# Latent attention with a dense layer on one core: rotary rows off GpSimd, block 0's side work dealt by a table

## The chip, the core and the metric

The kernel runs on one core of a Trainium2 chip. A core has five engines that run side by side and wait for each other through semaphores: TensorE (PE in the profile; its weight loads are PEld), VectorE (DVE), ScalarE (ACT), GpSimd (POOL) and SyncE (SP), which here only issues transfers. TensorE reads SBUF and writes PSUM; GpSimd works on SBUF alone in this kernel. The metric is the device time of one execution in microseconds. Shown for the kernel before are three runs: 1577.43, 1583.23 and 1586.42 us, median 1583.23.

## The reference, cut to what matters

One sequence of 2048 tokens with 512 features goes through an attention layer whose queries and keys come from low-rank latents, then through a dense layer. Both are followed by a residual and a layer norm.

```python
cq  = rms_norm(x @ w_qa.T, q_a_ln_w)              # 2048 x 384
q   = (cq @ w_qb.T)                               # 16 heads of 128 (nope) + 64 (pe)
q_pe = q_pe * cos + rotate_half(q_pe) * sin
ckv = x @ w_kva.T                                 # 2048 x (128 + 64)
k_pe = rope(ckv[..., 128:])                       # one, shared by all heads
kv  = rms_norm(ckv[..., :128], kv_a_ln_w) @ w_kvb.T   # per head 128 (k_nope) + 128 (v)
scores = (q_nope . k_nope + q_pe . k_pe) * 192 ** -0.5, causal
out = softmax(scores) @ v @ w_o.T
x = layernorm(x + out)
x = layernorm(x + x @ (weight * scale_weight[:, None]).T + bias)
```

The kernel never forms the keys and values of a head. It multiplies `w_qb` by the key half of `w_kvb` (`weights_q`), so a query meets the normalized latent itself, and it does the value half of `w_kvb` together with `w_o` after the softmax. Almost every operand is kept as a high and a low half in 16 bits, so that a product is made of three matmuls (high with high, high with low, low with high).

## The kernel before

**Blocks, pairs, tiles.** The queries are four blocks (b = 0 to 3) of 512. In a block, `units` goes over eight pairs of heads (p), and in a pair over four query tiles of 128 (qt). A tile of block b sees nk = (4b + qt + 1) * 128 keys. In block 0, where nk is at most 512, `pair_scores` makes the scores of both heads at once, takes the maxima (VectorE), the exponentials (ScalarE), and the reciprocal of the sum. `pair_probs` scales them and splits them into high and low halves (`hl`), and a transposing transfer brings them into `PT`. `values` multiplies the latent values by `PT` some tiles later; `lag` says how many tiles (3 in block 0). In blocks 1 to 3, `head_scores` and `head_probs` do the same for one head at a time, with scores in up to two pieces.

**Side work in block 0.** While block 0's tiles run, the rest of the inputs is still to be projected. `rest_of_x` projects the other twelve groups of 128 tokens (`project_x`: products, norm, transposes, store) and then, in `late_keys`, splits the rotated keys for all later blocks. `rest_of_w` prepares the query weights of three further groups of four heads (`weights_q`). Both are generators. Their steps, and those of the fillers (`project_pe` and `project_nope`, which make the next pair's queries), are taken in `units` at fixed places: one filler before each tile's scores, one step of `rest_of_x` in every tile but qt = 1, one step of `rest_of_w` in every tile of the first five pairs.

**Rotary part of the queries.** For a group g of four heads, `rope_products` multiplies and weighs with cosine and sine into `prod`. `rope_split` subtracts and adds (lines 504 and 505), and makes the high half by ScalarE and the low half (lines 507 to 512). `rope_stack` (line 521) then copies 32-row pieces so that the four heads' high and low rows stand under each other: 16 copies of 32x512 for a group. Block 0 gives the copies of the high rows to GpSimd and those of the low rows to VectorE; later blocks give all to GpSimd, except the first group of block 1, which VectorE does.

**Order.** TensorE's order is always the order of the program. In block 0 and to the start of block 3 a scheduler sets the order on VectorE, ScalarE and GpSimd. From the second tile of block 3 on, VectorE and ScalarE too run in program order. SP runs in program order from block 1 on. PSUM in block 0 has two buffers for scores and four (`m`) that all side products share: `ps_kv`, `ps_cq`, their transposes, `ps_wq`, `ps_qn`, `ps_pe`, `ps_tot` and the values' `o`. A product can only start when the buffer four products back has been read.

**Where the change touches.** In `kv_products`, `kvr` is a copy of a product of 256 columns (line 326), and GpSimd multiplies its second half by the cosine and sine table (`rot`, line 331) and adds (`kp`, line 334). `kv_finish` scales by the inverse norm on GpSimd (`nk`, line 340). `project_x` copies the query latent out of PSUM (`nq`, line 422) and scales it on GpSimd (line 424); before block 0's tiles the same is done from PSUM on VectorE (`cq_finish`, line 359). The inverse norm itself is two small GpSimd operations (lines 287 and 288). The low half of the inputs is a GpSimd subtraction (`xl`, line 308).

## Time and profile before

| what | value |
|---|---|
| runs shown, median (lowest to highest) | 1583.23 us (1577.43 to 1586.42) |
| the profiled execution | 1588.19 us, its span 1586.4 us |
| TensorE busy | 1500.4 us, 95% |
| VectorE busy | 1165.4 us, 73% |
| ScalarE busy | 923.7 us, 58% |
| GpSimd busy | 377.2 us, 24% |
| block 0's first scores, first maxima | 52.84 us, 53.71 us |
| block 1's first scores | 282.04 us |
| the last tile's exponentials end, output stage begins | about 1328 us |

The span has four stretches: the preparation up to block 0's first scores (0 to 53 us), block 0 with the side work (53 to 282 us), blocks 1 to 3 (282 to 1328 us), and the output stage (1328 to 1586 us). A line of the profile's groups names the line of the program, the engine, the operation, what is written and read with shapes, how often, the busy time in us and the mean of one in ns, and then the idle time ahead of it with what ended that. A line of the waits names who waited, for whom, the total in us, how often, and the longest. In a table of stretches each engine's busy time and number of instructions stand after the length of the stretch; PEclk is the granted TensorE clock, where 1.00 is full speed.

### The profile page before, as it was taken

What the parts mean: (1) busy time and instruction counts of PE and PEld (TensorE: products, weight loads), DVE (VectorE), ACT (ScalarE), POOL (GpSimd) and SP (SyncE); (2) the same over time, 40 slices, a digit from 0 to 9 for tenths busy, and PEclk for the clock granted to TensorE, in tenths of its full rate; (3) what the DMA queues carried; (4) which work ended last, traced back from release to release, by engine and by line L of the source; (5) the groups of instructions that cost most, each with busy time, mean ns of one, the idle gap of its engine ahead of it and who ended that gap; (6) DMA issues with size and microseconds to landing.
All of it is one profiled execution on the core that took longest, in us unless ns stands there. A gap on an engine that the chain in (4) does not pass through costs nothing. (4 is left out here: it accounts for less than half of the span.)

```text
span 1586.4 us, 24549 instructions
## 1 busy us (share of the span) xinstructions
PE 1500.4 (95%) x9100; PEld 1007.0 (63%) x9100; DVE 1165.4 (73%) x2124; ACT 923.7 (58%) x1668; POOL 377.2 (24%) x490
## 2 busy tenths in 40 slices
PE   8788887999999899999998999999999998999998
PEld 6667654566666566666665666566566666788876
DVE  4767787888878888888886777677677775465554
ACT  5566565666666676767765666666666665311120
POOL 5556531421405404040032400400400000022132
PEclk9999899999999999999999999999999999999999
DMA  5275455698889687978886788688688798433230
GB/s 203 76 181 163 113 128 135 123 173 153 161 180 176 128 170 151 164 150 163 161 189 122 145 154 159 129 154 161 119 153 168 159 228 198 144 118 122 93 113 34
DMA packets 614872, 234.56 MB, mean 148 GB/s; under 512 B 569696, under 2 KB 593248, under 8 KB 614112
## 3 DMA queue, kind: packets, MB, share of 16 engines
q1 hardware_dynamic: 613440, 231.26, 68.0%
q8 instruction: 71, 1.16, 0.3%
q10 hardware_dynamic: 1008, 1.18, 0.3%
q0 software_dynamic: 304, 0.56, 0.2%
q14 instruction: 49, 0.40, 0.1%
HBM read 62.33 MB, written 28.05 MB: 57 GB/s over the span
## 5 line engine op out<-in xcount | busy, mean ns | idle before, releaser
L596 PE MATMUL s<-Kn,qn 128*128 128x512 f16 (+5 forms) x1920 | 466.1, 349 | 20.6 <-ACT pr L648 20.3
L648 ACT ACTIVATE pr<-s,bias,er 128x1024 f32<-128x1024 f32 (+3 forms) x320 | 324.1, 1015 | 227.4 <-DVE bias L642 172.3
L725 PEld LDWEIGHTS <-V 128*128 128x128 f16 x3264 | 321.2, 99 | 94.5 <-issue 20.3
L672 DVE SCALAR_TENSOR_TENSOR hl<-pr,inv,hl 128x1024 f16<-128x1024 f32 (+7 forms) x320 | 350.8, 1110 | 34.4 <-ACT hl L669 28.9
L725 PE MATMUL o<-ring,V 128*128 128x256 f16 x3024 | 361.0, 273 | 0.0
L596 PE MATMUL s<-Kp,pe 128*128 128x512 f16 (+5 forms) x1280 | 342.4, 349 | 0.0
L669 ACT ACTIVATE hl<-pr,inv 128x1024 f16<-128x1024 f32 (+7 forms) x320 | 294.1, 960 | 76.7 <-ACT pr L648 33.9
L633 DVE TENSOR_REDUCE neg<-s 128x1 f32<-128x1024 f32 (+3 forms) x320 | 317.5, 992 | 24.0 <-PE s L596 20.6
L596 PEld LDWEIGHTS <-qn 128*128 128x128 f16 x1920 | 188.4, 98 | 173.8 <-issue 29.7
L596 PEld LDWEIGHTS <-pe 128*128 128x128 f16 x1280 | 125.3, 98 | 107.3 <-issue 1.3
L521 POOL COPY pe<-ph 32x512 f16<-32x512 f16 (+1 forms) x216 | 162.3, 751 | 26.8 <-ACT ph L511 11.8
L1013 PE MATMUL acc<-wvo,oh 128*128 128x512 f32 x448 | 144.8, 404 | 2.0 <-ACT pr L648 2.0
L554 PE MATMUL ps_qn<-cq,wq 128*128 128x512 f16 (+1 forms) x594 | 141.4, 386 | 5.6 <-DVE qn L69 2.8
L504 POOL TENSOR_TENSOR prod<-prod 128x512 f32<-128x512 f32 x15 | 19.0, 1268 | 525.1 <-DVE prod L499 525.1
L660 DVE TENSOR_SCALAR inv<-sums 128x1 f32<-128x1 f32 x128 | 27.1, 212 | 109.6 <-ACT pr L648 109.0
L554 PEld LDWEIGHTS <-wq 128*128 128x128 f16 x594 | 60.0, 101 | 69.6 <-issue 15.3
L1013 PEld LDWEIGHTS acc<-wvo,oh 128*128 128x128 f32 x448 | 83.6, 189 | 23.8 <-issue 4.1
L1013 PE MATMUL acc<-wvo,ol 128*128 128x512 f32 x224 | 88.5, 395 | 0.0
L494 PE MATMUL ps_pe<-cq,wpe 128*128 128x512 f16 (+1 forms) x306 | 69.8, 376 | 4.1 <-DVE nq L359 2.7
L730 ACT ACTIVATE ot<-o 128x256 f32<-128x256 f32 x128 | 48.2, 377 | 36.6 <-PE o L725 35.2
L74 ACT ACTIVATE oh<-o 128x1024 fp32r<-128x1024 f32 x28 | 29.7, 1059 | 64.3 <-PE acc L1013 48.6
L75 DVE TENSOR_TENSOR ol<-o,oh 128x1024 fp32r<-128x1024 f32 x28 | 38.8, 1386 | 37.9 <-ACT oh L74 37.9
(177 smaller groups left out, 1617.6 us busy)
## 6 DMA issues: line engine op xcount, KB each, us to landing
ot_d<-ot SPq DMA_DIRECT2D x128, 128.0 KB, 2.3
o<-ot_d SPq DMA_DIRECT2D x32, 512.0 KB, 3.7
wq<-wq_d SPq DMA_DIRECT2D x30, 384.0 KB, 3.7
wpe<-wpe_d SPq DMA_DIRECT2D x15, 384.0 KB, 3.8
wo<-in_wo_dram SPq DMA_DIRECT2D x4, 1024.0 KB, 5.5
x<-in_x_dram SPq DMA_DIRECT2D x16, 256.0 KB, 4.1
out_dram<-xb SPq DMA_DIRECT2D x16, 256.0 KB, 2.0
xr<-in_xT_dram SPq DMA_DIRECT2D x12, 256.0 KB, 4.3
```

Source lines behind the costliest of these rows:

```text
L75: nc.vector.tensor_tensor(l, ps, h.bitcast(F32), ALU.subtract)
L494: nc.tensor.matmul(ps, w[:, i, lt, x * P : (x + 1) * P], cq[:, k, lt, cols], start=n == 0, stop=n == 3 * LT - 1)
L521: engs[i].tensor_copy(pe[r : r + 32, j, cols], ph[q, i, x, cols])
L554: nc.tensor.matmul(ps, w[:, i, lt, j * P : (j + 1) * P], cq[:, k, lt, cols], start=n == 0, stop=n == 3 * LT - 1)
L596: nc.tensor.matmul(ps[:, :w], lhs, K[:, i, c0 : c0 + w], start=n == 0, stop=n == 4)
L633: nc.vector.tensor_reduce(neg[:, ti : ti + 1], v, axis=AX.XY, op=ALU.max, negate=True)
L648: nc.scalar.activation(pr[:, c0 : c0 + n * w].rearrange("p (a c) -> p a c", a=n), v, AF.Exp, bias=bias, scale=r, accum_out=sums[:, ti : ti ...
L669: nc.scalar.activation(hl[:, 0, c], pr[:, c], AF.Copy, scale=inv)
L672: nc.vector.scalar_tensor_tensor(hl[:, 1, c], pr[:, c], inv, hl[:, 0, c], ALU.mult, ALU.subtract)
L725: nc.tensor.matmul(ps[:, :256], vt[:, i, k % 4, :], v[:, :, l, k, :], start=n == 0, stop=n == 3 * kts - 1)
L730: nc.scalar.activation(ot, ps[:, :256], AF.Copy)
L1013: nc.tensor.matmul(acc, l[:, t, c], state["wvo"][p][:, i, j, :], start=p == 0 and j == 0 and n == 0, stop=p == NPAIR - 1 and j == 1 and n ...
```

## The change

Four things are changed together.

1. `kv_products`, `kv_finish` and `project_x` no longer pass through GpSimd: `rot` is multiplied by VectorE straight from PSUM and `kvr` is half as wide; `nk` is scaled by ScalarE; `nq` is scaled by VectorE from PSUM (`cq_finish`) after the norm is known, instead of copied first. GpSimd keeps the inverse norms, `xl`, and the small additions of `kp`.
2. `rope_split` runs on VectorE in blocks 1 to 3 (additions and low half); block 0 keeps its additions on GpSimd. `rope_stack` becomes a generator. In block 0 and for the first group of block 1, VectorE does all copies at once. In later groups ScalarE copies the high rows and VectorE the low rows, three copies after each head's scores (`move_rows`).
3. Before block 0's tiles: the rotary weights are loaded earlier and their squares taken earlier; each query tile's norm is made by itself; one query product is moved ahead of the column totals; the first products of the next weight group and the next split of x are moved between the two halves of the first queries, from after them; all of these use the four PSUM buffers `x`.
4. In block 0 a table `plan` says for each tile which steps to take (F a filler, X a step of `rest_of_x`, W a step of `rest_of_w`), after its scores; the probabilities of a tile are finished at once instead of after the next tile's scores; values run four tiles behind instead of three.

```diff
 def weights_q(g, direct=None, k="m"):
+    for lt in range(LT if direct is not None else 0):
+        nc.scalar.activation(junk[:, :256], rpe[:, lt], AF.Square, scale=qln[:, lt : lt + 1], accum_out=...)
...
-        kvr = pa2.tile([P, 256], F32, tag="kvr", name="kvr")
-        nc.vector.tensor_copy(kvr, ps[:, :256])
+        kvr = pa2.tile([P, P], F32, tag="kvr", name="kvr")
+        nc.vector.tensor_copy(kvr, ps[:, :P])
...
-        nc.gpsimd.tensor_tensor(rot, kvr[:, P:256].rearrange("p (a d) -> p a d", a=2), csk[:, i], ALU.mult)
+        nc.vector.tensor_tensor(rot, ps[:, P:256].rearrange("p (a d) -> p a d", a=2), csk[:, i], ALU.mult)
...
-        nc.gpsimd.tensor_scalar(nk, kvr[:, :P], rk, None, ALU.mult)
+        nc.scalar.activation(nk, kvr, AF.Copy, scale=rk)
...
-            nq = pa2.tile([P, LT * P], F32, tag="nq", name="nq")
-            nc.vector.tensor_copy(nq, pc)
             rk = inverse_rms(ms)
-            nc.gpsimd.tensor_scalar(nq, nq, rk[:, 1:2], None, ALU.mult)
+            nq = cq_finish(pc, rk[:, 1:2])
...
-    def rope_stack(pe, ph, cols, js, engs):
+    def rope_stack(pe, ph, cols, js, high):
         for j in js:
             q = slice(32 * j, 32 * j + 32)
-            for i in range(2):
-                for x in range(2):
-                    r = 64 * i + 32 * x
-                    engs[i].tensor_copy(pe[r : r + 32, j, cols], ph[q, i, x, cols])
+            for x in range(2):
+                yield high(pe[32 * x : 32 * x + 32, j, cols], ph[q, 0, x, cols])
+                yield nc.vector.tensor_copy(pe[64 + 32 * x : 96 + 32 * x, j, cols], ph[q, 1, x, cols])
+
+    def scalar_copy(dst, src):
+        return nc.scalar.activation(dst, src, AF.Copy)
+
+    stack = []
+
+    def move_rows(n=99):
+        while n and stack:
+            if next(stack[0], None) is None:
+                stack.pop(0)
+            else:
+                n -= 1
...
-        rope_split(b, prod, ph, every, (nc.gpsimd, nc.gpsimd), nc.gpsimd if b else nc.vector)
+        rope_split(b, prod, ph, every, (nc.vector, nc.vector) if b else (nc.gpsimd, nc.gpsimd), nc.vector)
...
+        later_rows = b and (b, g) != (1, 0)
+        stack.append(rope_stack(pe, ph, every, range(4), scalar_copy if later_rows else nc.vector.tensor_copy))
+        if not later_rows:
+            move_rows()
...
+    nc.sync.dma_start(wpe_r, a["wpe"][:, :, 0])
     nc.sync.dma_start(wk0, a["wk"][:, 0:4])
     nc.sync.dma_start(wqb_r, a["wqb"][0])
     nc.sync.dma_start(x_r[1], a["xT"][1])
     nc.sync.dma_start(csk[1], a["csk"][1])
-    nc.sync.dma_start(wpe_r, a["wpe"][:, :, 0])
...
+        def query(hb, i):
+            pc = cq_products(hb, i, x[hb], wqa, "x", msq[hb][:, i : i + 1])
+            return cq_finish(pc, inverse_rms(msq[hb][:, i : i + 1], 1)[:, 0:1])
...
         turn_queries(0, nqs, "x")
+        nqs = [query(1, 0)]
         next(w0)
         key_scales(0, 4)
         exp_scale(0, slice(0, 1))
-        nqs = queries(1)
-        next(w0)
+        nqs.append(query(1, 1))
...
             if hb == 0:
                 for _ in w0:
                     pass
-        next_x(2)
+                for _ in range(LT):
+                    next(w1)
+                next_x(2)
...
+    plan = (
+        ("WWF", "WFX", "WX", "X"),
+        ("FW", "FWF", "FXW", "W"),
+        ("FXW", "FW", "XW", "X"),
+        ("FW", "FWF", "FXW", "W"),
+        ("FXW", "FW", "XW", "X"),
+        ("FX", "FF", "FX", "X"),
+        ("FX", "FX", "X", "X"),
+        ("FX", "FX", "FFX", "X"),
+    )
...
-        lag = min(ring.shape[1] // (2048 * (b + 1)) - 1, 3) if b else 3
+        lag = min(ring.shape[1] // (2048 * (b + 1)) - 1, 3) if b else 4
...
                 if nk <= 512:
-                    fill()
                     pi = pair_scores(pool, b, p, qt, nk)
-                    flush()
                     probs.append(pair_probs(pool, b, p, qt, nk, PT, *pi))
-                    if qt != 1:
-                        next(side[0], None)
-                    if p < 5:
-                        next(side[1], None)
-                    if p + qt == 0:
-                        next(side[1], None)
+                    flush()
+                    for step in plan[p][qt]:
+                        if step == "F":
+                            fill()
+                        else:
+                            next(side[step == "W"], None)
                     run_values(lag)
                     run_values(lag)
...
+                        move_rows(3)
                         if 2 * qt + j in at:
                             fill()
```

## The prediction

> **What bounds the kernel now.** I read the page's engine shares first, then the table of stretches, then TensorE's waits, stretch by stretch, and last the groups and timelines of the operations that the change moves.
>
> ```profile
> PE 1500.4 (95%) x9100; PEld 1007.0 (63%) x9100; DVE 1165.4 (73%) x2124; ACT 923.7 (58%) x1668; POOL 377.2 (24%) x490
> ```
> ```profile
> core 0: us, PE busy (x) PEld busy (x) DVE busy (x) ACT busy (x) POOL busy (x), PEclk, DMA share, GB/s
> 0.00:53.00 53.00, 43.74 (x264) 36.79 (x265) 30.59 (x80) 29.82 (x85) 24.84 (x51) 0.97 0.49 165
> 53.00:201.00 148.00, 122.81 (x800) 94.36 (x797) 106.24 (x226) 93.08 (x269) 87.18 (x129) 0.91 0.52 138
> 201.00:282.00 81.00, 65.07 (x414) 39.98 (x415) 63.22 (x149) 48.10 (x126) 18.60 (x18) 0.90 0.57 134
> 282.00:866.00 584.00, 571.66 (x3658) 358.38 (x3656) 487.81 (x970) 400.92 (x688) 143.51 (x154) 0.99 0.82 160
> 866.00:1328.00 462.00, 447.46 (x2836) 278.97 (x2836) 346.19 (x502) 296.83 (x435) 52.90 (x57) 0.99 0.79 153
> ```
>
> TensorE is the bound, but not everywhere alike. From 282 us on it is busy 98% and 97% of the stretch at a clock of 0.99. In block 0 (53 to 282 us) it is idle for 25.2 + 15.9 us, and its clock is granted at 0.91 and 0.90 only: 13.3 + 8.1 us more in which no work was done. So some 62 of these 229 us are open to better order, and in blocks 1 to 3 only 27 us of 1046. The waits say what is late:
>
> ```profile
> PE o L725 <- DMA PT<-hl: 15.3, 4, 5.1
> PE ps_kv L316 <- POOL xl L308: 6.8, 1, 6.8
> PE ps_kt L379 <- DVE qn L69: 4.4, 1, 4.4
> PE ps_tot L165 <- DVE kvr L326: 4.3, 1, 4.3
> ...
> PE ps_qt L372 <- POOL nq L424: 2.7, 2, 2.4
> PE ps_pe L494 <- DVE nq L359: 2.7, 1, 2.7
> ```
> The four waits for transposed probabilities lie between 219 and 281 us, where the side work has run out; the one for `xl` ends at 60.76 us. GpSimd never bounds the span, but it holds the others up. The same VectorE copy of rotary rows, with GpSimd copying beside it (105 us) and with GpSimd idle (270 us):
>
> ```profile
> L521 DVE COPY pe<-ph x8: 286/492/636, 105.6 to 109.2; 32x512 f16<-32x512 f16 x8
> ```
> ```profile
> L521 DVE COPY pe<-ph x16: 274/284/289, 270.1 to 276.3; 32x512 f16<-32x512 f16 x16
> ```
>
> A copy takes 0.284 us alone and 0.492 beside GpSimd's. In the groups, GpSimd's own price is 0.776:
>
> ```profile
> L521 POOL COPY pe<-ph 32x512 f16<-32x512 f16 x200 | 155.2, 776 | 19.1 <-PE o L725 6.0 <-ACT ph L511 4.7
> L521 DVE COPY pe<-ph 32x512 f16<-32x512 f16 x40 | 16.2, 404 | 0.6
> ```
>
> **The change, part by part.** The sum is made against the profiled execution, 1588.2 us (span 1586.4), which is 5.0 us or 0.3% above the median of the runs, 1583.2.
>
> *Preparation (0 to 53 us).* TensorE's waits there that end on late norms and totals are 1.9 us (totals at 28.03), 2.7 (first rotary product at 36.29) and 1.5 (first weight product at 48.11); the clock of 0.97 costs 1.6. Together 7.7. A query product moved ahead of the totals covers the first; single norms free a PSUM buffer sooner. Against it: two more pairs of small GpSimd operations (0.23 + 0.72 us each), three squares of 0.51 + 0.19 us ahead of the sums they belong to, and on SP the rotary weights (0.39 MB) ahead of four other loads. Between +4 and -7.7; I take -4, about half, since each wait has a second cause close behind.
>
> *First split of x.* `xl` waited behind eight GpSimd copies (55.45, 3.92 us). Now no copy is on GpSimd, the split is asked for a half earlier, and the key product that reads it stands after two tiles' scores. The 6.8 us go, and with them half of the clock lost around 58 to 65 us (0.89 and 0.77 in two stretches of 10 us, 3.4 us). Between 0 and -10.2; I take -9, because some 10 us of TensorE work now stand ahead of that product, and the split needs 2.5 on GpSimd and 1.1 on ScalarE.
>
> *Rest of the first four pairs (to 201 us).* Idle 25.2 - 6.8 = 18.4 us and clock 13.3 - 3.4 = 9.9: 28.3 in all. What is removed: twelve hops of `nq` over GpSimd (1.40 us each), sixteen of `nk` (0.70) and of `rot` (0.46), and 24 + 16 rotary copies. What is added on VectorE: 24 copies of 32x512 at 0.284 and 16 of 32x256 at 0.22 (10.3 us), and `rot` from PSUM, 16 at about 0.28 (4.5, estimated from the 0.42 of 256 columns), less 2.2 for the shorter `kvr`. Its own old copies get cheaper by about the same as this: 24 from 0.46, 16 from 0.44, and other VectorE work that overlaps GpSimd's shrinks too. I put VectorE's net at 0. ScalarE gains 16 `nk` at 0.31 = 5 us, beside 93 busy of 148. The two longest waits (4.3 at 110.90, 4.4 at 182.63) do not vanish by this: both end when VectorE reads a side product behind a run of eight rotary copies (3.86 and 3.54 us); the run is now sixteen, 4.5 us. What helps them is that fewer side products are crowded into a tile. `nq` keeps its PSUM buffer about 1 us longer, until the norm (0.22 + 0.72) is known; queued behind it are the weight product and the values that take the next of the four buffers. Between +8 (three longer runs, twelve longer holds half covered) and -28.3; I take -13.
>
> *Last four pairs (to 282 us).* Idle 15.9 and clock 8.1: 24.0. Probabilities are now finished in their own tile and read four tiles later, so a transfer has some four tiles of 5 us instead of two. A new wait: each transposing transfer must stay back until the values of four tiles before have read the same buffer, late in its own tile; behind it on SP stand stores of `ot` and loads of x and weights. That leaves still more than three tiles. But side work now lies here too, and it brings VectorE and ScalarE work: VectorE is already busy 63 of 81 us. What is late next is the chain maximum, exponential, split, with two score buffers. Between 0 and -24; I take -13.
>
> *Blocks 1 to 3.* Per group VectorE gets two additions (0.69, the price of a 512 column operation, row 499), the low half (1.25) and eight copies (0.284): 4.9 us, for eleven groups 54, and 2.6 for the first. Less what GpSimd's overlap costs VectorE now: I estimate 18 us from durations with and without it. ScalarE gets 88 copies at about 0.63 (its 512 column row): 55 us. Room: VectorE idle 212 us, ScalarE 348 us of 1046. ScalarE also stops waiting for GpSimd's additions, which delay the exponentials at about 991 us and cost TensorE 2.9 us at 999.72. Between -8 (those waits go) and +55 (every ScalarE copy on the path, below); I take +4.
>
> [...]
>
> Sum: -4 - 9 - 13 - 13 + 4 = -35, so 1553 for an execution like the profiled one, 1548 beside the median. I forecast 1552. Output stage unchanged.
>
> **The rivals.** (a) *VectorE takes over block 0.* It is busy 200 us of the first 282 and idle for 82. If its work is unchanged and its idle time shrinks only by what it waits for TensorE and for `nk` now (some 10), the gain is 10 and the blocks give 4 back: 1582, or 1577 beside the median. For it: three bursts of sixteen copies. Against: the waits of the last pairs were for transfers, not for VectorE. (b) *Slower: the copies lengthen the head's loop in blocks 1 to 3.* In block 3 a head's chain, exponential, inverse, split, low half, maximum, bias, closes at 6.6 us (exponentials at 998.37 and 1005.00), as long as TensorE's work for it, and ScalarE's copies enter right before the split, where it waited only 0.53 us. All 88 exposed would cost 55, the sum 1604. It decides from 39 / 0.63 = 62 exposed copies on. Against it: the lag is made up once per pair, where a filler gives TensorE 4 us of other work and VectorE waits again. (c) *Nearly all goes.* All of block 0's loss: -7.7 - 10.2 - 28.3 - 24 + 4 = -66, 1522. Against it: VectorE would be busy nearly throughout.
>
> **How the numbers follow.** The forecast has 0.63, (a) 0.16, (b) 0.11, (c) 0.10. A difference under 0.5% (8 us) can't be told from none here. (a) lies at that edge: 0.05 faster, 0.10 same, 0.01 slower. So faster 0.63 + 0.10 + 0.05 = 0.78, same 0.10, slower 0.12. The range for 8 in 10 leaves out (b) and most of (c): 1527 to 1582; the forecast alone runs from 1535 to 1570.
>
> **What would show it.** Right: block 1's first scores near 244 to 252 us instead of 282; no TensorE wait for transposed probabilities; no wait for `xl` at 60 us; a clock near 0.95 in block 0; VectorE's rotary copies at 0.285 in the mean; blocks 1 to 3 within 10 us of 1046. Wrong: waits of TensorE for VectorE's reads of side products that add up to over 25 us in block 0, which is (a); waits for exponentials well over 20 us after block 0, which is (b).

## The result and the profile after

The changed kernel takes 1594.69 us (median of five executions, 1590.60 to 1596.43) against 1580.63 us for the kernel before on the same chip: a ratio of 1.0081, 95% interval 1.0054 to 1.0108. It is slower by 0.8%, and the prediction of 1552 us, faster by 2%, is wrong on both counts: outside its range and on the wrong side.

The profiled execution is the median one, with a span of 1592.8 us. The engines' busy times on its page:

```profile
PE 1501.2 (94%) x9100; PEld 1007.1 (63%) x9100; DVE 1197.0 (75%) x2304; ACT 982.2 (62%) x1772; POOL 123.4 (8%) x198
```

TensorE's work is the same. GpSimd has lost 254 us of its 377; VectorE has gained 32 and ScalarE 58. The table of stretches of the changed kernel, cut at the same times as the one in the prediction (engines with busy us and instructions, then the granted clock, the DMA share and GB/s):

```profile
0.00:53.00 53.00, 43.59 (x252) 35.31 (x253) 29.06 (x90) 32.12 (x94) 18.90 (x40) 0.94 0.50 172
53.00:201.00 148.00, 129.56 (x848) 98.94 (x848) 113.14 (x281) 101.00 (x290) 38.23 (x66) 0.92 0.59 147
201.00:282.00 81.00, 68.28 (x443) 43.32 (x441) 67.15 (x168) 50.65 (x128) 8.42 (x10) 0.95 0.57 135
282.00:866.00 584.00, 566.20 (x3599) 354.23 (x3598) 497.16 (x1035) 432.47 (x740) 6.39 (x2) 0.99 0.80 157
866.00:1328.00 462.00, 439.50 (x2792) 272.99 (x2791) 352.71 (x525) 304.70 (x446) 0.00 (x0) 0.99 0.78 151
```

Up to 282 us TensorE does 10 us more work in the same time than before: that is the gain. From 282 to 1328 us it is busy 13.4 us less than before (1005.7 against 1019.1), which means idle time that was not there. The same is seen in the times at which each block's first scores start:

| kernel | block 1 | block 2 | block 3 | first output product | end |
|---|---|---|---|---|---|
| before | 282.0 | 508.4 | 849.9 | 1323.7 | 1586.4 |
| after | 264.9 | 512.0 | 852.5 | 1332.8 | 1592.8 |

These are single executions. The one of the kernel before took 1588.2 us, 7.6 above its median, and a second kernel with the very instruction order of the changed one (experiment 6) has its blocks' times within 2.1 us of the changed kernel's (block 3's within 0.1), so smaller differences between two profiles say nothing.

Block 1 begins 17 us earlier (17 where the prediction wanted 30 to 38) and is over 3.6 us later: all that block 0 won has gone in block 1, 226.4 us long before and 247.1 now. Block 3 adds 6.5. TensorE's waits of the changed kernel from 282 to 1328 us (who waited, for whom, us in total, times, longest):

```profile
PE s L609 <- ACT pr L661: 26.4, 21, 2.9
PE o L738 <- DMA ring<-hl: 4.8, 2, 3.7
PE ps_qn L567 <- ACT ot L743: 4.6, 2, 2.3
PE ps_qn L567 <- DVE qn L69: 2.8, 1, 2.8
```

In the kernel before, the same stretch has

```profile
PE s L596 <- ACT pr L648: 20.3, 14, 5.3
PE ps_qn L554 <- DVE qn L69: 2.8, 2, 2.3
```

and the second and third of the four did not exist in it beyond 0.9 us. What ScalarE does just before one of them, as a timeline (start us, us, what, and in brackets the idle time ahead):

```profile
344.15 1.04 ACT L511 ACTIVATE ph<-prod 128x1024 f16<-128x1024 f32 x1
345.22 5.10 ACT L526 ACTIVATE pe<-ph 32x512 f16<-32x512 f16 x8
350.35 0.99 ACT L661 ACTIVATE pr<-s,bias,er 128x768 f32<-128x768 f32 x1
351.24 0.19 ACT L661 ACTIVATION_READ_ACCUMULATOR pr<-s,bias,er 128x1 f32 x1
351.33 0.68 ACT L68 ACTIVATE qn<-ps_qn,kvq 128x512 f16<-128x512 f32 x1
351.90 0.38 ACT L743 ACTIVATE ot<-o 128x256 f32<-128x256 f32 x1
```
```profile
352.33 1.89 PE L567 MATMUL ps_qn<-cq,wq 128*128 128x512 f16 x8 [2.31 <-ACT ot L743]
```

Eight row copies of 0.64 us stand in one run; the exponential, the high half of a query projection and the copy of values out of PSUM queue behind them, and TensorE's next product waits for that last copy. The table that deals three copies to a head is not what sets this: on ScalarE and VectorE a scheduler orders the instructions by itself up to block 3, and it put all eight together.

So the first theory was: T, the later groups' rotary work costs some 26 us by ScalarE's copies, and the rest of the change gains 12. Its rivals: A, block 0's new order leaves work to block 1's start; B, VectorE's additions and low halves are what costs.

### The profile page after: what moved, and what is told of

Read it like the earlier page. It is cut to its first block, busy times and chain, and to the rows that moved or that the text cites. A ratio compares the mean times of both kernels' runs of the same rounds, so it can differ in the third digit from the quotient of the medians.

```text
span 1592.8 us, 24492 instructions
## 1 busy us (share of the span) xinstructions
PE 1501.2 (94%) x9100; PEld 1007.1 (63%) x9100; DVE 1197.0 (75%) x2304; ACT 982.2 (62%) x1772; POOL 123.4 (8%) x198
## 5 line engine op out<-in xcount | busy, mean ns | idle before, releaser
L685 DVE SCALAR_TENSOR_TENSOR hl<-pr,inv,hl 128x1024 f16<-128x1024 f32 (+7 forms) x320 | 333.1, 1054 | 28.9 <-ACT hl L682 25.7
L74 ACT ACTIVATE xt<-tp 128x512 fp32r<-128x512 f32 x16 | 9.6, 598 | 91.3 <-PE tp L1139 68.9
L615 DVE TENSOR_TENSOR s<-s,maskb 128x128 f32<-128x128 f32 x160 | 46.7, 292 | 21.8 <-PE s L609 21.1
## 6 DMA issues: line engine op xcount, KB each, us to landing
o<-ot_d SPq DMA_DIRECT2D x32, 512.0 KB, 3.6
```

The source lines that it names most:

```text
L74: nc.scalar.activation(h, ps, AF.Copy)
L615: nc.vector.tensor_tensor(dg, dg, maskb, ALU.add)
L685: nc.vector.scalar_tensor_tensor(hl[:, 1, c], pr[:, c], inv, hl[:, 0, c], ALU.mult, ALU.subtract)
```

## The experiments

Each time is a median, and each ratio is against the kernel before on the same chip (medians of 1580.6 to 1583.0 us). Differences between two kernels are differences of their ratios, times 1581 us, with the two half-intervals added as squares. In all diffs "-" is the changed kernel unless the kernel before is named. Two of the expectations speak of 32 row copies in a group; a group has 16, 8 high and 8 low.

### 1. The later groups' rotary work put back

```diff
-        rope_split(b, prod, ph, every, (nc.vector, nc.vector) if b else (nc.gpsimd, nc.gpsimd), nc.vector)
+        rope_split(b, prod, ph, every, (nc.gpsimd, nc.gpsimd), nc.gpsimd if b else nc.vector)
...
-        stack.append(rope_stack(pe, ph, every, range(4), scalar_copy if later_rows else nc.vector.tensor_copy))
-        if not later_rows:
-            move_rows()
+        eng = nc.gpsimd if later_rows else nc.vector
+        stack.append(rope_stack(pe, ph, every, range(4), eng.tensor_copy, eng.tensor_copy))
+        move_rows()
```

> The changed kernel with the rotary work of the later groups (blocks 1 to 3) back where it was: additions and low halves on GpSimd, all 32 row copies of a group at once on GpSimd (the first group of block 1 on VectorE). Block 0 and the preparation stay changed. Theory T (the dealt ScalarE copies stand in front of exponentials and of the copies that free PSUM): block 1 goes from 247 us back to 226-230, block 3 from 480 to 474, so 1594.7 - 20 - 6 = 1569 us (1564-1576), faster than both kernels. Rival A (block 0's new order and the lag of four leave work to block 1's start, the copies are hidden): block 1 stays at or above 240 us and the time at or above 1588.

Measured: 1577.49 us, ratio 0.9970 (0.9958 to 0.9982). Block 1 takes 234.1 us, block 3 472.6. Part 2 of the change costs 17.6 ± 4.7 us, so its direction is as T had it; but what is left of the change gains 5 us, not 12. The time lies just above T's range, and block 1's lies between T's and A's.

### 2. The later groups' rotary work alone

The kernel before with part 2 of the change and block 0 as it was ("-" is the kernel before):

```diff
-        rope_split(b, prod, ph, every, (nc.gpsimd, nc.gpsimd), nc.gpsimd if b else nc.vector)
+        rope_split(b, prod, ph, every, (nc.vector, nc.vector) if b else (nc.gpsimd, nc.gpsimd), nc.vector)
...
+            stack.append(rope_stack(pe, ph, every, range(4), scalar_copy if later_rows else nc.vector.tensor_copy))
...
+                        move_rows(3)
```

> The kernel before with only the rotary work of blocks 1 to 3 changed. T: block 0 as before (229 us), block 1 up by 15-20 us, block 3 up by 6, in all 1580.6 + 24 = 1605 us (1596-1612). Rival A: within 4 us of the kernel before (1577-1585). Rival C, that the loss needs both the changed block 0 (which ends earlier and so leaves block 1 a shorter start) and the dealt copies: between, 1585-1595, with block 1 up by less than 10 us.

Measured: 1610.14 us, ratio 1.0185 (1.0163 to 1.0208). Block 1 takes 242.7 us and block 3 481.5. That is T's range. Rival A falls as the main cause, since the loss is there with block 0 unchanged; a smaller part of it comes back in experiment 9.

### 3. and 4. Which engine, and which part of the work

All row copies of the later groups on VectorE, dealt as before:

```diff
-        stack.append(rope_stack(pe, ph, every, range(4), scalar_copy if later_rows else nc.vector.tensor_copy))
+        stack.append(rope_stack(pe, ph, every, range(4), nc.vector.tensor_copy))
```

> The changed kernel with all row copies of the later groups, still dealt three to a head, on VectorE, none on ScalarE. T: the gaps in front of which ScalarE ran six to eight copies of 0.64 us go; VectorE takes 16 x 0.29 = 4.6 us more for each of 11 groups, part of it in the way: 1582 us (1573-1588). Rival B (what costs is VectorE's added work, the additions and low halves at 1.2 us a piece, not ScalarE's copies): 1595-1606.

Measured: 1607.66 us, ratio 1.0167 (1.0144 to 1.0190), 14 us worse than the changed kernel. Additions and low half back on GpSimd, copies dealt over ScalarE and VectorE:

```diff
-        rope_split(b, prod, ph, every, (nc.vector, nc.vector) if b else (nc.gpsimd, nc.gpsimd), nc.vector)
+        rope_split(b, prod, ph, every, (nc.gpsimd, nc.gpsimd), nc.gpsimd if b else nc.vector)
```

> The changed kernel with the additions and the low half of the later groups back on GpSimd, the row copies still dealt over ScalarE and VectorE. T: ScalarE's runs of copies stay where they were, so 1590-1598 us with block 1 at 240 us or more. Rival B: the loss goes with VectorE's additions: 1570-1580.

Measured: 1619.66 us, ratio 1.0239 (1.0219 to 1.0258), 25 us worse than the changed kernel. T falls by experiment 3: with ScalarE's copies moved to VectorE the kernel is slower, where T wanted it faster, so it is not ScalarE's queue as such. B came near there (1595 to 1606), but falls by experiment 4: without VectorE's additions the kernel is slower, where B wanted 1570 to 1580. The groups of this last kernel, 282 to 1328 us (busy us, mean ns, then idle time ahead and what ended it), point to why the two together are worst:

```profile
L523 DVE COPY pe<-ph 32x512 f16<-32x512 f16 x88 | 25.2, 286 | 5.4 <-POOL ph L512 3.8
...
L512 POOL TENSOR_TENSOR ph<-prod,ph 128x1024 f16<-128x1024 f32 x11 | 23.4, 2129 | 13.3 <-ACT ph L511 13.3
```

VectorE's copies, in order on its queue, now wait for GpSimd's low half, and what stands behind them on VectorE waits too: TensorE's waits for `qn` on VectorE are 13.2 us in this stretch, against 2.8 in the changed kernel.

### 5. The additions on VectorE, the copies on GpSimd

```diff
-        stack.append(rope_stack(pe, ph, every, range(4), scalar_copy if later_rows else nc.vector.tensor_copy))
-        if not later_rows:
-            move_rows()
+        eng = nc.gpsimd if later_rows else nc.vector
+        stack.append(rope_stack(pe, ph, every, range(4), eng.tensor_copy, eng.tensor_copy))
+        move_rows()
```

> The changed kernel with only the additions and the low half of the later groups on VectorE; all 32 row copies of a group at once on GpSimd, as before. Both theories of the runs so far fell (row copies on VectorE instead of ScalarE cost 13 us more, additions back on GpSimd 25 us more), so the next is theory D: what costs is the 32 copies in two queues that also carry the exponentials and the splits, three a head and the rest in one run of 14 at the end of each even pair; the additions themselves cost VectorE 2.6 us a group and hide. D: 1577 us (1571-1584), block 1 at 231-237. Theory V, that VectorE has no room for anything in these blocks: 1588-1600.

Measured: 1569.77 us, ratio 0.9920 (0.9902 to 0.9938). Part 2 is two things of opposite sign. The additions and the low half on VectorE gain 7.9 ± 3.4 us (against experiment 1); the row copies on ScalarE and VectorE lose 25.5 ± 5 (the changed kernel against this one). The two are not independent: by way of experiment 4 the copies lose 42.5 ± 3.6 and the additions then gain 25.0 ± 5.3. The signs are the same both ways. The time lies just below theory D's range. TensorE's waits for exponentials from 282 to 1328 us fall from 26.4 us in the changed kernel to

```profile
PE s L609 <- ACT pr L661: 17.4, 16, 3.3
```

and GpSimd's own copies, in the groups of this kernel over the same stretch, are

```profile
L522 POOL COPY pe<-ph 32x512 f16<-32x512 f16 x88 | 75.7, 860 | 568.1 <-ACT ph L511 503.9 <-PE o L738 61.0
...
L523 POOL COPY pe<-ph 32x512 f16<-32x512 f16 x88 | 70.6, 802 | 4.2
```

A copy takes GpSimd 0.80 to 0.86 us, three times VectorE's 0.286, a group some 13 us. But the rows are wanted only at the next even pair of heads, and little else stands on GpSimd's queue. On VectorE or ScalarE the same copies stand ahead of a maximum, an exponential or a copy out of PSUM that TensorE wants at once; for ScalarE the timeline at 345 us shows it, for VectorE it is inferred from the times of experiments 3 and 12.

### 6. An edit that did nothing

> The changed kernel with its row copies dealt over two pairs: what three a head have not moved by the end of an even pair is moved in the next pair's heads, not in one run (they are due only at the pair after that). D with the run as the cost: the gaps at 309, 352, 411 and 501 us and the half clock after them go, block 1 at 232-238 instead of 247, block 3 at 480 still, 1583 us (1577-1588). D with each copy at its price wherever it stands: block 1 at 243 or more, 1592-1600 us.

```diff
-        move_rows()
+        if flush_rows:
+            move_rows()
...
-            drain()
+            drain(p % 2 == 1)
```

The edit let copies stay over the end of an even pair. Six heads at three copies each already take all 16, so none was left over, and the order of the instructions was that of the changed kernel. Measured: 1597.30 us, ratio 1.0098 (1.0067 to 1.0128). It serves as a repeat of the changed kernel (1.0081) and says nothing on the runs.

### 7. Whole runs, or each copy

ScalarE's copies are held behind what the program writes before them on ScalarE, so that the scheduler can't gather them:

```diff
     def scalar_copy(dst, src):
-        return nc.scalar.activation(dst, src, AF.Copy)
+        return tc.keep_in_program_order(nc.scalar.activation(dst, src, AF.Copy))
```

> The changed kernel with ScalarE's row copies held behind what is written before them on ScalarE. (The run on two pairs left the instructions in the very order of the changed kernel: a group has 16 copies, not 32, and six heads take them all; the runs of six and eight are the scheduler's, which orders ScalarE and VectorE by itself up to block 3.) Now ScalarE's runs in blocks 1 and 2 are of one or two. If the runs cost: the gaps behind them in block 1 (3.7, 2.3, 2.3, 2.8 us) and the half clock after them go, block 1 at 231-237 us and 1582 us (1577-1587). If each copy costs wherever it stands: 1591-1598.

Measured: 1593.66 us, ratio 1.0070 (1.0055 to 1.0085). ScalarE's runs in block 1 are now of one or two copies, the waits behind them are gone and block 1 takes 236.6 us instead of 247.1. But block 3 takes 4.3 us more (block 2 1.8, no more than a repeat can differ by); a wait of 6.08 us for an exponential stands at block 3's start. The whole is the changed kernel's time within the interval. So block 1 did what was expected if the runs cost, and the whole what was expected if each copy costs wherever it stands. The opposite, all sixteen at once behind the split, shows in block 3, where order is the program's:

```diff
         stack.append(rope_stack(pe, ph, every, range(4), scalar_copy if later_rows else nc.vector.tensor_copy))
-        if not later_rows:
-            move_rows()
+        move_rows()
```

> The changed kernel with the 16 row copies of a later group written at once behind its split, on ScalarE and VectorE as in the change. If the dealing is what costs: block 3 at 470-475 instead of 480 and 1585-1590 us. If the engines are what costs, ScalarE has a run of 5.1 us and VectorE one of 2.3 for each of block 3's three groups: block 3 at 480-490, 1595-1605.

Measured: 1601.57 us, ratio 1.0128 (1.0113 to 1.0143), block 3 482.5 us against 480.3. Dealing is no loss; it may help by 7 ± 5 us. What loses is that the copies run on these two engines.

### 8. Each engine's share

The low rows back on GpSimd, the high rows dealt on ScalarE; and the other half, high rows on GpSimd, low rows dealt on VectorE:

```diff
+        if later_rows:
+            for _ in rope_stack(pe, ph, every, range(4), None, nc.gpsimd.tensor_copy):
+                pass
+            stack.append(rope_stack(pe, ph, every, range(4), scalar_copy, None))
...
+            for _ in rope_stack(pe, ph, every, range(4), nc.gpsimd.tensor_copy, None):
+                pass
+            stack.append(rope_stack(pe, ph, every, range(4), None, nc.vector.tensor_copy))
```

> The changed kernel, but the low rows of the later groups (8 of 16 copies) on GpSimd at once; the high rows stay dealt on ScalarE. Against 1569.8 with all on GpSimd and 1594.7 with eight on ScalarE and eight on VectorE. Cost by time of the copies (0.627 to 0.286): ScalarE's eight carry 17 of the 25 us: 1587 us (1582-1592). Cost by VectorE, which is busy most of block 1: 1573-1580.

> The other half: high rows of the later groups on GpSimd at once, low rows dealt on VectorE. Cost by time of the copies: 1578 us (1573-1582). Cost by VectorE: 1585-1592. If the two halves add up to less than 25 us over 1569.8, the loss needs both queues held at once.

Measured: 1599.22 us, ratio 1.0103 (1.0088 to 1.0118), and 1589.27 us, ratio 1.0041 (1.0025 to 1.0057). Against experiment 5:

| copies of the later groups (the rest on GpSimd) | their busy time, us | cost, us | exposed |
|---|---|---|---|
| 88 on ScalarE | 55.1 | 28.9 ± 3.7 | 52% |
| 88 on VectorE | 25.2 | 19.1 ± 3.8 | 76% |
| 88 and 88, the changed kernel | 80.3 | 25.5 ± 5 | 32% |
| 176 on VectorE (experiment 3) | some 50 | 39.1 ± 4.6 | 78% |

Experiment 11 meets neither of its expectations. Experiment 12 falls in the range "cost by VectorE", which experiment 11 rules out as the only cause, and the two halves add up to more than 25 us, not less. On VectorE twice as many copies cost twice as much; but the shares of the two engines don't add. The block times fit the reading that VectorE's copies go into time in which it waits for a late ScalarE: the kernel with ScalarE's copies alone has block times of 247.0, 341.7 and 480.3 us, and the changed kernel 247.1, 340.5 and 480.3.

### 9. Block 0's order

Experiment 1's kernel with the old order of block 0 (no table, probabilities flushed a tile late, values three tiles behind):

```diff
-        lag = min(ring.shape[1] // (2048 * (b + 1)) - 1, 3) if b else 4
+        lag = min(ring.shape[1] // (2048 * (b + 1)) - 1, 3) if b else 3
...
+                    fill()
                     pi = pair_scores(pool, b, p, qt, nk)
+                    flush()
                     probs.append(pair_probs(pool, b, p, qt, nk, PT, *pi))
-                    flush()
-                    for step in plan[p][qt]:
...
+                    if qt != 1:
+                        next(side[0], None)
+                    if p < 5:
+                        next(side[1], None)
+                    if p + qt == 0:
+                        next(side[1], None)
```

> The kernel with the later groups undone (1577.5 us), and block 0's order back as before as well: one projection step ahead of the scores, probabilities flushed one tile late, side steps by the old rule, values three tiles behind. If the order is worth what the prediction gave it (the four waits for transposed probabilities, 15 us and the half clock behind them): 1590 us (1584-1597), block 1's first scores near 278. If the order only moves work from block 0 to block 1's start: 1574-1582.

Measured: 1578.61 us, ratio 0.9977 (0.9967 to 0.9987): the order is worth 1.1 ± 2.5 us there. This is the second branch of the expectation, and the two profiles show it. With the old order block 1's first scores start at 273.4 us instead of 265.9, but block 1 then takes 226.2 us instead of 234.1: what the order wins in block 0 is lost at block 1's start. In experiment 1's kernel TensorE waits there three times for VectorE, which still has the first group's row copies of block 1 to do (`pe`):

```profile
267.53 0.71 PE L609 MATMUL s<-Kp,pe 128*128 128x320 f16 x2 [1.10 <-DVE pe L523]
...
278.90 1.14 PE L738 MATMUL o<-qn,V 128*128 128x256 f16 x9 [1.86 <-DVE prod L502]
...
282.28 4.00 PE L567 MATMUL ps_qn<-cq,wq 128*128 128x512 f16 x9 [2.23 <-DVE inv L671]
```

None of the three is in the kernel with the old order. To this extent rival A was right. The same lines the other way, the new order put into the kernel before, alone:

> The kernel before with only block 0's table of steps, probabilities finished in their own tile, and values four tiles behind. If the order only moves idle time from block 0's end to block 1's start: 1578-1583, block 1's first scores near 270 and block 1 at 234. If it is worth the prediction's -13: 1568 (1563-1573).

Measured: 1568.58 us, ratio 0.9918 (0.9903 to 0.9932): it is worth 13.0 ± 2.3 us here. That this is the prediction's figure for the last four pairs is luck, since the order also removes the wait for `xl`, which the prediction had in another term. The difference is shared with something else in the change.

### 10. Block 0's work off GpSimd

Part 1 of the change alone in the kernel before, the norms, `rot` and `nk` and all of block 0's row copies; then all but the last pair of lines below (and the two like it in the preparation), without the row copies ("-" is the kernel before):

```diff
-        kvr = pa2.tile([P, 256], F32, tag="kvr", name="kvr")
-        nc.vector.tensor_copy(kvr, ps[:, :256])
+        kvr = pa2.tile([P, P], F32, tag="kvr", name="kvr")
+        nc.vector.tensor_copy(kvr, ps[:, :P])
...
-        nc.gpsimd.tensor_tensor(rot, kvr[:, P:256].rearrange("p (a d) -> p a d", a=2), csk[:, i], ALU.mult)
+        nc.vector.tensor_tensor(rot, ps[:, P:256].rearrange("p (a d) -> p a d", a=2), csk[:, i], ALU.mult)
...
-        nc.gpsimd.tensor_scalar(nk, kvr[:, :P], rk, None, ALU.mult)
+        nc.scalar.activation(nk, kvr, AF.Copy, scale=rk)
...
-            nc.gpsimd.tensor_scalar(nq, nq, rk[:, 1:2], None, ALU.mult)
+            nq = cq_finish(pc, rk[:, 1:2])
...
-            engs = (nc.gpsimd, nc.vector)
+            engs = (nc.vector, nc.vector)
```

> The kernel before with only the work of block 0 and the preparation taken off GpSimd: the norms of queries and keys, the product with the key's rotary factors, and all row copies of block 0 (on VectorE). By difference of the runs so far -6.7 us: 1575 us (1571-1579). If the parts of block 0 help only together: 1579-1583. By the prediction's own share for the first four pairs (-9 and -13): 1560.

> The kernel before with the norms and the product with the key's rotary factors taken off GpSimd, all row copies as before. The two parts together gained 6.7 us. If the 40 row copies on VectorE lose 4 to 6 us also without the order: 1570 us (1567-1573). If they lose only under it: 1573-1577.

Measured: 1574.28 us, ratio 0.9955 (0.9940 to 0.9970), 7.1 us gained, and 1576.17 us, ratio 0.9962 (0.9948 to 0.9976), 6.0 us gained. So parts 1 and 4, worth 7.1 and 13.0 alone, are worth only 8.2 ± 3.3 together (experiment 11, where the preparation's first row copies stay on GpSimd): some 12 ± 5 are missing. TensorE's waits between 40 and 285 us name the larger part. The norms alone:

```profile
PE o L723 <- DMA PT<-hl: 14.1, 4, 5.0
PE ps_kt L379 <- DVE qn L69: 7.0, 2, 3.6
PE ps_kv L316 <- POOL xl L308: 6.9, 1, 6.9
```

The order alone:

```profile
PE ps_wq L226 <- DVE qn L69: 8.2, 2, 4.2
PE o L725 <- DMA PT<-hl: 5.8, 1, 5.8
PE ps_tot L165 <- ACT junk L230: 5.4, 1, 5.4
PE ps_tot L165 <- ACT junk L388: 4.2, 1, 4.2
PE ps_qt L372 <- POOL nq L424: 3.9, 2, 2.8
```

The wait for `xl`, 6.9 us and a half clock of 6.8 us around its end, of which 4.7 fall on work and cost 2.4, is still there with the norms alone. It goes when the row copies leave GpSimd, and it goes just as well when the order puts other products ahead of the one that reads `xl`. With both, it can only go once. In the kernel with the norms and the rows off GpSimd, that wait is gone too, yet the time is that with the norms alone within 1.1 us (± 3.2): the 40 copies moved to VectorE would then have cost about what the wait was worth. Their cost was not measured apart. The expectation read such a time as copies that cost something only under the order; that the wait is gone without a gain speaks against this. Some 4 of the 12 lie in block 1, which takes 226.1 us with the order alone, 227.6 with part 1 alone and 231.7 with both (226.4 in the kernel before).

### 11. The preparation, and what is best

Experiment 1's kernel with the preparation of before (the loads, the squares, the queries, the steps of the second weight group, the first row copies):

```diff
-        nqs = [query(1, 0)]
         next(w0)
         key_scales(0, 4)
         exp_scale(0, slice(0, 1))
-        nqs.append(query(1, 1))
+        nqs = queries(1)
+        next(w0)
...
-                for _ in range(LT):
-                    next(w1)
-                next_x(2)
+        next_x(2)
         state["wq", 0, 1] = wq0[1]
+        w1 = weights_q(1)
+        for _ in range(LT):
+            next(w1)
```

> The kernel with the later groups undone, and the preparation (the order of queries, totals, rotary squares, the four loads, the first row copies, the steps of the second weight group) back as before. First scores at 53 us instead of 57, and the wait of 5.2 us for the first query projection gone: 1573 us (1568-1577) if the 4 us are kept to the end; 1576-1582 if the four steps of weights that now lie behind the first scores take them back.

Measured: 1573.30 us, ratio 0.9948 (0.9927 to 0.9968): the new preparation costs 3.5 ± 3.7 us. The same edit on experiment 5's kernel:

> Additions and low half on VectorE with all 16 row copies of a group on GpSimd (1569.8 us), and the preparation as before (worth 4.2 us in the run before this one, 1577.5 to 1573.3). If both gains add: 1565.6 us (1562-1569). If they take the same slack: 1569-1573.

Measured: 1560.16 us, ratio 0.9856 (0.9835 to 0.9878), 10.1 ± 4.5 us better than experiment 5. From that kernel, block 0's 24 high-row copies of 32x512 were given back to GpSimd:

```diff
-        stack.append(rope_stack(pe, ph, every, range(4), eng.tensor_copy, eng.tensor_copy))
+        high = eng if b else nc.gpsimd
+        stack.append(rope_stack(pe, ph, every, range(4), high.tensor_copy, eng.tensor_copy))
```

> The fastest kernel so far (1560.2 us) with block 0's high rows, 24 copies, on GpSimd as before, so that VectorE's runs in pairs 1 to 6 are of eight and not of sixteen. If the runs of sixteen set the waits for low halves of query projections in front of the weight products (3.8 us at 99.9 and 3.3 at 158.2 us): those halve and 1556 us (1552-1559). If GpSimd's longer copies beside VectorE's cost as much: 1559-1565.

Measured: 1553.77 us, ratio 0.9825 (0.9808 to 0.9841): 4.9 ± 4.3 us more, and the fastest of all, 1.75% under the kernel before. Its engines:

```profile
PE 1490.9 (96%) x9100; PEld 1004.2 (65%) x9100; DVE 1173.5 (76%) x2176; ACT 926.6 (60%) x1684; POOL 295.5 (19%) x410
```

The gain came, but not where it was expected: the two waits for weight products are still 4.3 and 3.9 us long. What went are the waits of 2.3 us at 117 and 176 us and those at block 1's start (2.1 and 1.8). Last, the order and the additions alone, which is this kernel less the norms ("-" is the kernel before with the new order, experiment 9):

```diff
-        rope_split(b, prod, ph, every, (nc.gpsimd, nc.gpsimd), nc.gpsimd if b else nc.vector)
+        rope_split(b, prod, ph, every, (nc.vector, nc.vector) if b else (nc.gpsimd, nc.gpsimd), nc.vector)
```

> The kernel before with block 0's order and with the later groups' additions and low half on VectorE, nothing else: the fastest kernel (1553.8 us) less the norms taken off GpSimd. The two gains alone are 12.4 and 8 us: 1561 us (1557-1565). If the norms are worth under the order what they are without it (some 7 us), it stands at 1561; if the order covers them too, at 1552-1556, and the interplay of block 0's parts is the norms'.

Measured: 1557.69 us, ratio 0.9843 (0.9822 to 0.9864). The norms off GpSimd are worth 2.8 ± 4.2 us under the order; most of the best kernel's gain is two of the edits, the order and the additions.

## Why the prediction was wrong

**The sum as measured.** Parts 1 and 4, block 0's: -8.2. Preparation: +3.5. Later additions: -7.9. Later row copies: +25.5. Together +12.9 us; the changed kernel is 12.8 us above the kernel before. These are steps along one path from kernel to kernel, so that they add up proves nothing; by another path a part can be worth something else (experiments 5 and 9). Block 0's three terms missed by 27 us, blocks 1 to 3 by 14, the preparation by 7.5. With block 0 as foreseen the change would still have been faster; with blocks 1 to 3 as foreseen, the same as before.

**Blocks 1 to 3, +4: the step that turned the sign.** Its bounds were right (-8 to +55) and so were its counts: 88 ScalarE copies at 0.627 us were foreseen at 0.63 and 55 us. What failed is the step "the lag is made up once per pair": it took these copies to lie beside TensorE's work because ScalarE was idle for 348 us and VectorE for 212 of 1046. Idle time of an engine in this loop is not free time: with the copies of one engine alone, half of ScalarE's and three quarters of VectorE's came out at the end. The term is +17.6, in two pieces: the prediction had the sign of the additions right (-7.9, at its lower bound of -8), and the copies' +25.5 too small.

**Rival (b)**, at a chance of 0.11, had the mechanism for ScalarE's copies, and gave VectorE's no price. It asked for 62 exposed copies because it set them against a gain of 39; against the 12.6 us that the other parts came to (8.2 - 3.5 + 7.9) it needs 20. It looked for the loss in block 3, in the program's order; more came in block 1 (16.2 us against experiment 5, 10.6 in block 3), where the scheduler had gathered the copies in runs of six to eight.

**First split of x, -9; rest of the first four pairs, -13; last four pairs, -13: the largest miss.** -35 was foreseen and 8 came. Alone in the kernel before, the parts do gain: the order 13, the work off GpSimd 7. The waits that the prediction listed for `xl` and for transposed probabilities went, or nearly: of the 15.3 us for the latter 2.7 are left. What failed is that little was put down for the waits next in line. TensorE's longest waits in the changed kernel between 40 and 285 us:

```profile
PE ps_wq L230 <- DVE qn L69: 8.4, 2, 5.1
PE s L609 <- DVE qn L69: 5.2, 1, 5.2
PE ps_kt L384 <- DVE qn L69: 4.6, 2, 2.3
PE ps_tot L165 <- ACT junk L393: 3.9, 1, 3.9
PE o L738 <- DMA PT<-hl: 2.7, 1, 2.7
```

For `ps_wq` 1.5 us were waited in the kernel before, and for the first scores nothing; `ps_kt` and `ps_tot` are about what they were (4.4 and 4.3). Two more things were missed. Some 4 to 8 us of what block 0 wins are lost at block 1's start (experiments 9 and 10), where the sum had no term. And the ceiling was too high: the prediction added all lost clock to all idle time, 62 us, but by the trace's clock records only 14.4 of its 21.4 us of lost clock fall on time in which TensorE worked, so some 55 were open, and at `xl` 8.7 at most instead of 10.2.

**Rival (a)**, at 0.16, had block 0 nearly: a gain of 10, and VectorE's idle time of 82 us shrinking by some 10; 8.2 came, and up to block 1's first scores VectorE is idle for 69 us of 265. But its sign, over 25 us of waits for VectorE in block 0, was not reached: from 53 to 265 us they are 20.6. That VectorE bounds block 0 is not shown.

**Preparation, -4.** Measured +3.5 and +10.1 on two kernels. TensorE's first scores stand behind a wait for VectorE's low half of the first query projection that the prediction did not list:

```profile
56.85 0.37 PE L609 MATMUL s<-Kn,qn 128*128 128x128 f16 x2 [5.16 <-DVE qn L69]
```

This is not what the new preparation costs, though: with the old one under the new order (experiment 11's first kernel) a wait of 5.23 us for the totals of the weights, behind ScalarE, stands at 53.19 us in its place.

**What it said would show.** No wait for `xl`: right. One wait of 2.7 us for transposed probabilities instead of none. VectorE's copies at 0.285 us: 0.286. The clock in block 0 at 0.95: 0.92 and 0.95. Block 1's first scores at 244 to 252 us: 264.9. Blocks 1 to 3 within 10 us of 1046: they grew by 26, and the waits for exponentials after block 0, (b)'s sign, from 20.3 us to 26.4.

**The rule of the Trainium skill.** The page "Perfetto Trace Analysis", section "Optimizing Scalar/DVE Operations", says that with a saturated VectorE offloading some work to ScalarE or even GpSimd may make sense; the change goes the other way. (VectorE is busy 73% here; whether that counts as saturated the page does not say.) By it the 57 us that the prediction reckoned for VectorE in blocks 1 to 3 would be a loss in full and its sum would end near 1606, an estimate; the result, 1595, is nearer to that than to 1552. But taken so, the rule was right only for the copies. VectorE's additions, by it a part of the loss, gained 7.9 us. The next section of the page, "Optimizing GPSIMD Operations", prefers other engines where possible, as GpSimd is generally slower. The copies are three times slower there, as it says, and still cheaper there by 25.5 us.

How the 25.5 us divide can be read from the two profiles: from block 1's first scores to the first output product the changed kernel takes 1067.9 us and TensorE is idle for 45.0 of them, experiment 5's 1037.5 and 22.6, so some three quarters are waits; most of the rest is half clock on work (12.0 and 5.3 us by the clock records). What stays open: how the loss divides between the two engines, whose shares do not add, and why the new preparation costs 3.5 ± 3.7 us with one kernel and 10.1 ± 4.5 with another, if the two differ at all.

## What to carry to other kernels

Ask of a piece of work not how long it takes on an engine but who waits for it and what stands behind it on that queue: slow copies that nobody wants soon belong on the idle engine, while additions in the middle of a chain between two other engines do not, even if the idle engine has room for both. Busy shares of 60 and 75% do not mean room, where the engines take turns in one loop. And before gains of several parts are added, list for each wait all the parts that remove it: it can be won only once, and the next wait in line, in this stretch or at the start of the next, decides what is left of it.

## What was not expected of the hardware

The clock was halved after some waits of 2.3 to 2.4 us, and not after others of the same length. In the changed kernel the stretches around a wait of 2.36 us that ended at 1002.69 us, and around one of 2.31 us that ended at 352.33 us, have these granted clocks (the figure behind POOL's busy time):

```profile
993.90:1003.90 10.00, 7.64 (x53) 4.98 (x52) 7.37 (x11) 5.64 (x9) 0.00 (x0) 1.00 0.51 109
1003.90:1007.40 3.50, 3.50 (x11) 1.39 (x10) 3.17 (x6) 2.83 (x4) 0.00 (x0) 0.51 1.16 217
1007.40:1017.40 10.00, 10.00 (x66) 6.14 (x64) 8.17 (x13) 6.48 (x10) 0.00 (x0) 1.00 0.53 105
342.00:352.30 10.30, 8.03 (x52) 4.95 (x51) 10.02 (x25) 8.75 (x15) 0.00 (x0) 1.00 0.89 168
352.30:355.70 3.40, 3.37 (x22) 2.15 (x22) 1.83 (x8) 3.40 (x6) 0.00 (x0) 1.00 0.00 0
```

The first wait was followed by 3.4 us at half speed, so it cost some 4.1 us instead of 2.4; the second by none. So the price of a wait of this length can't be read from its length alone. The trace's clock records show what it goes by. In both kernels, before and after, all half-clock stretches but the one that the span's end cuts off are 3.41 us long or two or three times that, and within a kernel they start whole multiples of 3.41 us apart: the clock is set anew on a fixed grid. Cut on that grid, the windows with the two waits and those behind them are:

```profile
348.59:352.00 3.41, 1.44 (x8) 0.64 (x7) 3.23 (x10) 3.36 (x7) 0.00 (x0) 1.00 0.61 154
352.00:355.41 3.41, 3.08 (x20) 1.90 (x20) 1.79 (x8) 3.41 (x8) 0.00 (x0) 1.00 0.00 0
1000.53:1003.94 3.41, 1.25 (x8) 0.78 (x8) 1.94 (x5) 2.59 (x5) 0.00 (x0) 1.00 0.14 29
1003.94:1007.35 3.41, 3.41 (x11) 1.34 (x9) 3.08 (x6) 2.79 (x4) 0.00 (x0) 0.50 1.15 216
```

In the window before 352.00 TensorE was idle for 1.97 us, since the wait reached 0.33 us into the next one; in the window before 1003.94 it was idle for 2.16. From 40 us on, in both kernels, each of the 23 full-speed windows that a half-speed one follows has at least 2.03 us of idle time, and no other full-speed window has over 1.97.
